# Self attention on one core: the place of the second piece of scores, of the exps, and the engine that copies first

## The chip, the cores and the metric

The kernel runs on one core of a Trainium2 chip. A core has engines that each work through a queue of their own, in order: TensorE (PE; its weight loads are listed as PEld) multiplies matrices, VectorE (DVE) and ScalarE (ACT) work on elements and can read the accumulation memory PSUM, GpSimd (POOL) works on elements in SBUF, and SyncE (SP) issues transfers. They wait for each other by semaphores only. The metric is the device time of one execution in microseconds (us), as a median over runs.

## The reference

An encoder of one layer over a short context (2 x 77 tokens), and a decoder of one layer over 2 x 2048 tokens: causal self attention, cross attention to the encoder's output, and a feed-forward part, each behind a layer norm and with a residual. All in fp32, width 512, 16 heads of 32. The change touches the decoder's self attention alone:

```python
yn = _ln(y, dec_n1_s, dec_n1_b)
y = y + _mha(yn, yn, ..., sb)          # self attention
...
# in _mha, with q, k, v of shape (2, 16, 2048, 32):
scores = jnp.einsum('bhqd,bhkd->bhqk', q, k) / jnp.sqrt(hd)
scores = scores + bias[None]           # relative bias, -inf above the diagonal
attn = jax.nn.softmax(scores, axis=-1)
out = jnp.einsum('bhqk,bhkd->bhqd', attn, v)
```

## The kernel before

The order of all work is written out by hand; no scheduler moves anything. Self attention is cut into 128 units (b, m, g, t): batch b (2), block m of 512 queries (4), group g of four heads (4), and tile t of 128 queries (4). A unit with index i = 4m + t attends to i + 1 tiles of 128 keys, its size: 1 to 4 in block m = 0, 5 to 8 in m = 1, 9 to 12 in m = 2, 13 to 16 in m = 3. The keys of a unit come in pieces of up to four tiles (`pieces`, L304); a size of 13 is cut 4, 4, 3, 2. Work goes through a stream of pieces, two pieces of one unit at a time (a pair).

For each pair, the loop at L1262 does this:

- It makes sure that the unit's scores and exps are issued (L1265 to L1268).
- `turn` (L397): PE transposes the probabilities of the pair, four 128 x 128 tiles into one PSUM bank (L411), and the bank is copied to SBUF as `pts`, by ACT (L417) or DVE (L415). In blocks m > 0 a bank holds one tile of keys for the four heads, so a full pair fills eight banks. The first half of the banks is copied by ACT, the second by DVE (L414). An exp of a later unit is issued behind the fourth bank (L418), and one more at the end (L420).
- If the pair ends its unit, `slot(n + 1)` runs the jobs of that place: a projection of q, k or v, or an output projection (L206, L217, L230, L242: eight matmul instructions each), the division by the softmax sums, and pieces of norm, encoder or cross attention. Their tables are fixed before (L896 to L928).
- One piece of scores is issued if it may be (L1280): its unit is at most two ahead, and writes over the probabilities of a unit whose tiles have been turned that far (`may_score`, L1244).
- One or two exps (L1282).
- `values` (L422): PE multiplies the turned tiles with v into bank 7 (L428).
- Further pieces of scores, as far as they may go, if the pair had two pieces or the block is m = 0 (L1285).

`scores` (L344) takes four banks, one a head; PE fills them with matmuls on 32 rows each (L361), and DVE empties them: without bias for far keys (L370), with the bias and mask for the last two tiles (L377), each with a running maximum, and when the last piece is done the negated maximum (L384). In blocks m > 0 the four exps of the unit (L387, ACT) are then put on a list, `late_exps`, from which `exps(k)` takes the oldest.

All banks but the one of `values` come from one rotation of seven (`bank`, L170): a stretch that asks for a bank gets the one that was asked for seven requests before, and waits until that has been emptied. A bank of transposes is released by its copy, a bank of scores by DVE.

Of the kernel before, what the change touches and what calls it, by code (L numbers as in the profile page):

```python
# [54 lines left out]
def tile_encoder_decoder(ctx: ExitStack, tc: tile.TileContext, ins, out):  # L55
# [93 lines left out]
    with (  # L149
# [20 lines left out]
        def bank():  # L170

            i = count["bank"] % count["banks"]
            count["bank"] += 1
            return psum[:, i, :]

        def in_turn(what, tile):
            i = count[what] % tile.shape[1]
            count[what] += 1
            return tile[:, i, :]
# [138 lines left out]
        units = [(b, m, g, t) for b in range(B) for m in range(NMB) for g in range(NC) for t in range(TB)]  # L318
# [20 lines left out]
        def exps(k):  # L339

            for _ in range(min(k, len(late_exps))):
                late_exps.pop(0)[1]()
# [54 lines left out]
        def turn(pieces):  # L397

            first = units[pieces[0][0]][1] == 0
            loads = []  # L400
            for n, k0, kn in pieces:
                ks = range(k0, k0 + kn)
                if first:
                    loads += [[(n, k, r) for k in ks] for r in range(HC)]
                else:
                    loads += [[(n, k, r) for r in range(HC)] for k in ks]
            for o, load in enumerate(loads):
                pt = bank()
                pts = in_turn("pts", pts_all).rearrange("p (x q) -> p x q", q=P)
                for x, (n, k, r) in enumerate(load):  # L410
                    nc.tensor.transpose(pt[:, ts(x, P)], state[n]["p"][r][:, ts(k, P)], ident)  # L411
                    got[n, k, r] = pts[:, x, :]
                w = len(load) * P
                if o % 2 if first else o >= (len(loads) + 1) // 2:  # L414
                    nc.vector.tensor_copy(pts[:, : len(load), :], pt[:, :w])  # L415
                else:
                    nc.scalar.copy(pts[:, : len(load), :], pt[:, :w])  # L417
                if o == min(3, len(loads) - 1):  # L418
                    exps(1)
            exps(1)  # L420

        def values(n, k0, kn):  # L422
            b, m, g, t = units[n]
            i = m * TB + t
            for k in range(k0, k0 + kn):
                ot = psum[:, 7, :].rearrange("p (t q) -> p t q", q=P)
                for r in range(HC):
                    nc.tensor.matmul(  # L428
                        ot[rows4(r), t, :], vv[:, k, ts(g * HC + r, HD)], got.pop((n, k, r)),
                        start=(k == 0), stop=(k == i),  # L430
                    )
                if t == TB - 1 and k == i:
                    o = ots[b, m, g] = in_turn("oT", oT_all)
                    (nc.vector.tensor_copy if m else nc.scalar.copy)(o, psum[:, 7, :])
# [461 lines left out]
        for x, (b, m) in enumerate(blocks):  # L896
            u = x * NU
            first = m == 0
# [77 lines left out]
        def slot(n):  # L976
            for f in light[n]:
                f()
            for _, run, _ in jobs[n]:
                load_next()  # L980
                run(loaded[ran[0]])
                ran[0] += 1
            if n == 5:
                load_next()
# [35 lines left out]
        def w_1_load(i):  # L1020

            nc.sync.dma_start(w_1[:, :, ts(i, D)], wchunk("dec_ff1_wT", i * D))
# [221 lines left out]
        def may_score():  # L1244

            if at[0] == len(stream):
                return False
            n, k0, kn = stream[at[0]]
            same = n >= 2 and units[n][:2] == units[n - 2][:2]
            return n < 2 or turned_to[n - 2] >= (min(k0 + kn, size[n - 2]) if same else size[n - 2])  # L1250

        def score_next():
            n, k0, kn = stream[at[0]]
            scores(n, k0, kn)
            scored_to[n] = k0 + kn
            at[0] += 1
# [5 lines left out]
        while i < len(stream):  # L1262
            n = stream[i][0]
            pair = [p for p in stream[i : i + 2] if p[0] == n]
            while scored_to.get(n) != size[n]:  # L1265
                score_next()
            while any(u == n for u, _ in late_exps):
                exps(1)  # L1268
            ends = pair[-1][1] + pair[-1][2] == size[n]
            if ends:  # L1270
                for f in ahead[n + 1]:
                    f()
            turn(pair)
            if n == end - 2:
                for _, k0, _ in pair:
                    w_1_load(k0 // 4)
            turned_to[n] = pair[-1][1] + pair[-1][2]
            if ends and n + 1 < end:
                slot(n + 1)
            if may_score():  # L1280
                score_next()
            exps(2 if units[n][1] == 1 else 1)  # L1282
            for p in pair:
                values(*p)
            while may_score() and (len(pair) > 1 or units[n][1] == 0):  # L1285
                score_next()
            i += len(pair)

        xt_ring += [sb.tile([P, D], F32, name="xt", tag="xt", bufs=2) for _ in range(2)]
# [71 lines left out]
```

## Time and profile before

| what | value |
|---|---|
| time, median of 3 runs | 2931.29 us (2929.42 to 2933.62) |
| profiled execution | 2935.85 us, of which its span is 2934.1 us |
| mean granted TensorE clock in it | 0.991 |
| PE busy | 2868.7 us (98%) |
| DVE busy | 2205.3 us (75%) |
| ACT busy | 1219.5 us (42%) |
| block m = 1, b = 1 (1058 to 1253 us) | PE 192.08, DVE 161.35, ACT 106.23 of 195 us |
| block m = 2, b = 1 (1253 to 1486 us) | PE 231.48, DVE 196.74, ACT 134.87 of 233 us |
| block m = 3, b = 1, without its end (1486 to 1720 us) | PE 231.22, DVE 199.88, ACT 142.73 of 234 us |
| behind self attention (1800 to 2934 us) | PE 1108.90, DVE 768.68, ACT 253.51 of 1134 us |

The span is cut by the blocks of self attention, which fill about the first 1780 us; the encoder and the first cross attention are spread between them. Busy time of PE is generous: matmuls overlap and their ends are modelled, so a PE that stands still for half a microsecond between two matmuls may be shown as busy. What PE lost is read from the distances between the starts of its rows in the timeline, and who ended a wait from the bracket at a row's end.

### The profile page before, as it was taken

Reading aid. Unit: us, or ns where it says so; the run is one execution under the profiler, and the core shown is the slowest. Engines: PE = TensorE matmul, PEld = TensorE weight load, DVE = VectorE, ACT = ScalarE, POOL = GpSimd, SP = SyncE. Lnnn points to the kernel's source line nnn. Section 1 sums busy time; section 2 is a strip of 40 time slices with the busy share of each in tenths; the row PEclk is TensorE's granted clock in tenths of the full one; section 3 lists DMA queues with packets and bytes.
Section 4 is the critical chain, followed back from the end, with each engine's and each line's share of the span. In section 5 each row is a group of like instructions: output and inputs, shape, how many; then the busy total and the mean of one; then the engine's idle time right before and its main releaser. Section 6 shows DMA issues by size and latency. Waiting matters only on the chain.

```text
span 2934.1 us, 60690 instructions
## 1 busy us (share of the span) xinstructions
PE 2868.7 (98%) x24440; PEld 2012.8 (69%) x24440; DVE 2205.3 (75%) x6171; ACT 1219.5 (42%) x2211; POOL 736.9 (25%) x601
## 2 busy tenths in 40 slices
PE   8899999999999999999999999999999899999999
PEld 5457666666666556666666667777777777777788
DVE  4767688878987788888888895767676767676765
ACT  3344456546665445565556672313131313131311
POOL 0100000000000101000000004555555464646465
PEclk9899999999999999999999999999999999999999
DMA  6413301201112502211101115000001000000000
GB/s 174 99 54 112 100 16 56 63 16 44 34 41 64 135 19 76 70 30 56 48 16 37 41 46 191 1 29 1 29 1 38 10 29 1 29 1 29 1 15 15
DMA packets 117644, 137.10 MB, mean 47 GB/s; under 512 B 18241, under 2 KB 73073, under 8 KB 117235
## 3 DMA queue, kind: packets, MB, share of 16 engines
q1 hardware_dynamic: 117362, 133.22, 15.7%
q8 instruction: 192, 3.15, 0.4%
q14 instruction: 90, 0.73, 0.1%
HBM read 111.33 MB, written 21.86 MB: 45 GB/s over the span
## 4 chain that ended last, share of the span: by engine, by line
PE 80%; DVE 13%; issue 2%; POOL 2%; ACT 2%; DMA 1%; SPq 0%; POOLq 0%; DVEq 0%; ACTq 0%
PE psum L1165 13%; PE psum L411 12%; PE psum L361 10%; PE psum L1134 8%; PE psum L428 7%; DVE pp L370 5%; PE psum L230 4%; PE psum L814 4%; PE psum L754 4%; PE psum L206 4%; PE psum L242 4%; PE psum L217 3%; DVE pp L377 3%; PE psum L794 2%; PE psum L805 1%
## 5 line engine op out<-in xcount | busy, mean ns | idle before, releaser
L387 ACT ACTIVATE pp<-pp,nm 128x128 f32<-128x128 f32 (+15 forms) x512 | 614.1, 1209 | 195.1 <-DVE nm L384 192.3
L370 DVE TENSOR_SCALAR_CACHE_REDUCE pp<-psum 128x512 f32<-128x512 f32 (+3 forms) x1024 | 558.0, 589 | 53.3 <-PE psum L361 51.5
L411 PE MATMUL psum<-ident,pp 128*128 128x128 f32 x4352 | 549.0, 279 | 18.0 <-DVE mx L377 11.8
L411 PEld LDWEIGHTS psum<-ident,pp 128*128 128x128 f32 x4352 | 474.5, 142 | 132.4 <-DVE pp L370 57.1
L417 ACT COPY pts<-psum 128x512 f32<-128x512 f32 (+3 forms) x592 | 298.7, 577 | 510.5 <-PE psum L411 401.3
L1117 POOL TENSOR_TENSOR vv<-pp 128x512 f32<-128x512 f32 x320 | 414.5, 1311 | 145.3 <-PE psum L1134 125.7
L361 PE MATMUL psum<-kT,q 32*128 32x512 f32 (+3 forms) x2560 | 353.5, 579 | 8.7 <-DVE mx L377 3.9
L415 DVE COPY pts<-psum 128x512 f32<-128x512 f32 (+2 forms) x544 | 329.9, 660 | 42.5 <-PE psum L411 40.8
L428 PEld LDWEIGHTS psum<-pts,vv 128*32 128x32 f32 x8704 | 226.2, 110 | 123.9 <-issue 116.9
L428 PE MATMUL psum<-pts,vv 128*32 128x128 f32 x8704 | 278.9, 276 | 0.0
L276 POOL TENSOR_TENSOR rstd<-rstd,mhalf 128x1 f32<-128x1 f32 x32 | 18.2, 570 | 919.9 <-DVE rstd L275 854.7
L1154 ACT ACTIVATE kT<-kT,vecs 128x256 f32<-128x256 f32 x256 | 115.2, 499 | 300.8 <-DVE kT L1151 300.8
L377 DVE CUSTOM_DVE_ANT_0 pp<-psum,bias 128x256 f32<-128x256 f32 (+1 forms) x512 | 209.6, 409 | 24.5 <-PE psum L361 16.6
L1151 DVE TENSOR_TENSOR kT<-kT,psum 128x512 f32<-128x512 f32 x256 | 166.4, 680 | 80.9 <-PE psum L1134 80.5
L361 PEld LDWEIGHTS psum<-kT,q 32*128 32x128 f32 x2560 | 119.6, 184 | 153.0 <-issue 99.3
L1165 PE MATMUL psum<-vv 128*128 128x256 f32 x768 | 176.9, 381 | 0.0
L1134 PE MATMUL psum<-oT,vv 128*128 128x256 f32 x736 | 166.5, 380 | 0.0
L1165 PEld LDWEIGHTS psum<-vv 128*128 128x128 f32 x768 | 143.1, 190 | 26.8 <-issue 9.5
L1134 PEld LDWEIGHTS psum<-oT,vv 128*128 128x128 f32 x736 | 138.8, 190 | 24.4 <-issue 6.2
L1117 DVE TENSOR_TENSOR vv<-kT 128x512 f32<-128x512 f32 x160 | 140.0, 892 | 10.8 <-PE psum L1165 9.8
L257 POOL TENSOR_TENSOR xr<-xr,row_dec_sa_out_b 128x512 f32<-128x512 f32 x30 | 38.1, 1274 | 375.1 <-DVE pts L415 244.3
L206 PE MATMUL psum<-nT,wqk 128*128 128x512 f32 x256 | 119.1, 609 | 0.0
(178 smaller groups left out, 3920.0 us busy)
## 6 DMA issues: line engine op xcount, KB each, us to landing
wqk<-in_dec_sa_in_wT_dram SPq DMA_DIRECT2D x64, 256.0 KB, 3.8
bias<-tz SPq DMA_DIRECT2D x128, 128.0 KB, 3.5
wbig<-in_dec_sa_in_wT_dram SPq DMA_DIRECT2D x8, 1024.0 KB, 7.3
vv<-in_enc_ff_wT_dram SPq DMA_DIRECT2D x8, 1024.0 KB, 5.4
wbig<-in_dec_sa_out_wT_dram SPq DMA_DIRECT2D x8, 1024.0 KB, 7.5
vv<-y SPq DMA_DIRECT2D x32, 256.0 KB, 3.5
out_dram<-vv SPq DMA_DIRECT2D x32, 256.0 KB, 2.0
xt<-in_x_dram SPq DMA_DIRECT2D x30, 256.0 KB, 3.9
```

What stands on the lines that cost most here:

```text
L206: nc.tensor.matmul(mm, w[:, c, :], nTs[b, m][:, c, :], start=(c == 0), stop=(c == NC - 1))
L361: nc.tensor.matmul(banks[r][:, : kn * P], q[rows4(r), ts(t, P)], kT[rows4(r), g, k0 * P : (k0 + kn) * P], start=True, stop=True,)
L370: nc.vector.tensor_scalar(p[:, k0 * P : (k0 + far) * P], s[:, : far * P], 1.0, None, ALU.mult, ALU.max, accum_out=st["mx"][:, r, c : c + 1],)
L377: nc.vector.tensor_tensor_reduce(p[:, (i + 1) * P - w : (i + 1) * P], s[:, far * P : kn * P], biases[b, m, g][:, r, 2 * P - w :], 1.0, LOW ...
L387: nc.scalar.activation(p, p, AF.Exp, bias=nm, accum_out=to)
L411: nc.tensor.transpose(pt[:, ts(x, P)], state[n]["p"][r][:, ts(k, P)], ident)
L415: nc.vector.tensor_copy(pts[:, : len(load), :], pt[:, :w])
L417: nc.scalar.copy(pts[:, : len(load), :], pt[:, :w])
L428: nc.tensor.matmul(ot[rows4(r), t, :], vv[:, k, ts(g * HC + r, HD)], got.pop((n, k, r)), start=(k == 0), stop=(k == i),)
L1117: engine.tensor_tensor(dst, quarter(*parts[0], n), quarter(*parts[2], n), SIGN[parts[1]])
L1134: nc.tensor.matmul(mm[:, ts(f, TOK)], a[:, c, ts(f, P)], b[:, c, :], start=(c == 0), stop=(c == 1))
L1165: nc.tensor.matmul(mm[:, t, :], lhs[:, c, ts(t, P)], rhs[:, c, :], start=(n == 0 and c == 0), stop=(n == 3 and c == 1),)
```

## The change

Two places are edited. In `turn`, for blocks m > 0, DVE copies the first half of the banks (rounded down) and ACT the rest, where ACT had the first half (rounded up) and DVE the rest; the number of copies of each engine stays. The exp that stood behind the fourth bank is left for block m = 0 only, so for m > 0 one exp instead of two is issued in `turn`, behind all copies. In the loop, the further pieces of scores come ahead of `values`, directly behind the first piece and its exps, and one exp is issued behind them.

```diff
@@ turn
                 w = len(load) * P
-                if o % 2 if first else o >= (len(loads) + 1) // 2:
+                if o % 2 if first else o < len(loads) // 2:
                     nc.vector.tensor_copy(pts[:, : len(load), :], pt[:, :w])
                 else:
                     nc.scalar.copy(pts[:, : len(load), :], pt[:, :w])
-                if o == min(3, len(loads) - 1):
+                if first and o == len(loads) - 1:
                     exps(1)
             exps(1)
@@ the loop over the stream
             if may_score():
                 score_next()
             exps(2 if units[n][1] == 1 else 1)
+            while may_score() and (len(pair) > 1 or units[n][1] == 0):
+                score_next()
+            exps(1)
             for p in pair:
                 values(*p)
-            while may_score() and (len(pair) > 1 or units[n][1] == 0):
-                score_next()
             i += len(pair)
```

## The prediction

> **What bounds the kernel now.** I read the page's busy times and chain first, then the busy time of each block, then one repeating stretch of block m = 3 row by row on PE, DVE and ACT. The page:
>
> ```profile
> PE 2868.7 (98%) x24440; PEld 2012.8 (69%) x24440; DVE 2205.3 (75%) x6171; ACT 1219.5 (42%) x2211; POOL 736.9 (25%) x601
> PE 80%; DVE 13%; issue 2%; POOL 2%; ACT 2%; DMA 1%; SPq 0%; POOLq 0%; DVEq 0%; ACTq 0%
> 1486.00:1720.00 234.00, 231.22 (x2722) 156.58 (x2715) 199.88 (x644) 142.73 (x199) 5.10 (x4) 0.99 0.12 37
> ```
>
> PE is the bound on average, but the chain goes over to DVE for 13%, and in block m = 3 (third line: length, then PE, PEld, DVE, ACT, POOL busy) DVE is busy for 85%. Such a DVE is not idle at every moment at which PE needs it. The repeating stretch, from the first score piece of one unit's second pair to the next such piece (start, length, line, count), PE:
>
> ```profile
> 1600.15 1.14 PE L361 MATMUL psum<-kT,q 32*128 32x512 f32 x8
> 1601.22 1.30 PE L428 MATMUL psum<-pts,vv 128*32 128x128 f32 x40
> 1602.45 0.93 PE L361 MATMUL psum<-kT,q 32*128 32x384 f32 x8
> 1603.31 4.47 PE L411 MATMUL psum<-ident,pp 128*128 128x128 f32 x32
> 1607.71 1.14 PE L361 MATMUL psum<-kT,q 32*128 32x512 f32 x8
> 1608.78 1.95 PE L428 MATMUL psum<-pts,vv 128*32 128x128 f32 x64
> 1610.66 1.14 PE L361 MATMUL psum<-kT,q 32*128 32x512 f32 x8
> 1611.73 2.84 PE L411 MATMUL psum<-ident,pp 128*128 128x128 f32 x24
> 1614.41 3.70 PE L217 MATMUL psum<-nT,wqk 128*128 128x512 f32 x8
> 1618.04 0.71 PE L361 MATMUL psum<-kT,q 32*128 32x512 f32 x4
> ```
>
> and DVE and ACT in the same stretch:
>
> ```profile
> 1601.31 0.69 DVE L370 TENSOR_SCALAR_CACHE_REDUCE pp<-psum 128x512 f32<-128x512 f32 x1 [0.30 <-PE psum L361]
> ...
> 1606.66 0.16 DVE L384 TENSOR_REDUCE nm<-mx 128x1 f32<-128x5 f32 x1
> 1606.74 2.48 DVE L415 COPY pts<-psum 128x512 f32<-128x512 f32 x4
> 1609.14 0.68 DVE L370 TENSOR_SCALAR_CACHE_REDUCE pp<-psum 128x512 f32<-128x512 f32 x1
> ...
> 1611.82 0.69 DVE L370 TENSOR_SCALAR_CACHE_REDUCE pp<-psum 128x512 f32<-128x512 f32 x1 [0.16 <-PE psum L361]
> ```
>
> ```profile
> 1604.00 2.05 ACT L417 COPY pts<-psum 128x512 f32<-128x512 f32 x4 [6.08 <-PE psum L411]
> 1605.91 1.93 ACT L387 ACTIVATE pp<-pp,nm 128x1920 f32<-128x1920 f32 x1
> ```
>
> The reader is to see that DVE runs without a gap from 1601.31 to 1611.58: eight evictions of scores, four copies, the next evictions. PE loses only 0.76 us here (transposes 4.40 from start to start, 3.64 where nothing waits, as at 1567.71): it always has something that needs no DVE. It is ACT's early copies that free banks 0 to 3 of the transposes, and `values` that fills PE while DVE empties the first piece.
>
> **The change, part by part.** *Fewer score stretches.* A piece of four key tiles takes 1.07 from start to start, one of three 0.86: 0.215 a tile and 0.21 a stretch beside. In the built order the stretches of L361 fall from 299 to 185, so at most 114 x 0.21 = 24 us are saved, where PE doesn't wait otherwise. A rule of the Trainium skill bears on this (TensorEngine Tiling (Array Packing), Key Properties): a change of tiling mode drains TensorE; by it alone the change would give 2931 - 24 = 2907. The same page (PSUM Bottleneck) warns that tiling speeds TensorE up but not the emptying of PSUM, for which both ScalarE and VectorE should be used; the rows here, 1.07 us to fill four banks and 2.45 us for DVE to empty them, agree with that one, and it speaks against two pieces in a row.
>
> *Copies and order in the first pair of a unit in m = 3.* On the clock of the rows above. With the second piece directly behind the first, `values` starts at 1600.15 + 0.86 + 0.65 + 0.21 = 1601.87, the transposes 0.21 earlier, at 1603.10. DVE's evictions keep their times and end at 1606.74. The seventh bank of transposes waits for the last of them, as before; the eighth takes the bank of the first one, now copied by DVE at 1606.74 + 0.60 (four copies fill 2.40), plus 0.07 to resume: transposes end at 1607.41 + 0.45 = 1607.86 (before 1607.71). The next score piece takes the banks of transposes 2 to 5. Three of these are now DVE's: free at 1607.94, 1608.54 and 1609.14, where ACT freed them by 1606. There is no projection in this place to cover it. Its third head starts at 1609.21. DVE evicts the first head when it is ready, 1.16 after its start (1600.15 to 1601.31), so from 1609.17, and frees it at 1609.78. The second piece's fourth head needs just that bank: 1609.85 + 0.86 + 0.21 = 1610.92. Only then `values` starts (before 1608.78); with 1.88 the transposes of the next pair start at 1612.80 instead of 1611.73: **1.07 us lost**. Queued behind the waiting scores on PE are `values`, the transposes and the projection; ACT waits for these transposes, DVE for the projection, where it has slack. Bounds: if the copies freed banks without delay, 1607.86 + 1.93 + 1.88 = 1611.67, 0.06 gained; if the two pieces don't overlap at all, 1609.21 + 1.07 + 1.07 + 1.88 = 1613.23, 1.5 lost. I take 1.07, since the rows show heads overlapping. The other three tiles t, with last pieces of 0.88 or 0.53 a head, give 1.0, 0.7 and 1.0 by the same steps; mean 0.95. Three groups a block are in this steady state: 2 x 12 x 0.95 = **+23**.
>
> *Block m = 2.* Here a first pair is often followed by two more pieces:
>
> ```profile
> 1405.19 0.93 PE L361 MATMUL psum<-kT,q 32*128 32x384 f32 x8
> 1406.05 1.96 PE L428 MATMUL psum<-pts,vv 128*32 128x128 f32 x64
> 1407.93 3.29 PE L361 MATMUL psum<-kT,q 32*128 32x512 f32 x16
> 1411.15 1.09 PE L411 MATMUL psum<-ident,pp 128*128 128x128 f32 x8
> ```
>
> The 3.22 of the third row is 1.29 over 2 x 0.86 + 0.21: DVE-bound already. Three pieces in a row need twelve banks of seven. DVE, continuous from its copies, evicts the first piece from about 1406.1 to 1409.1 and the first head of the second by 1409.7; the third piece's fourth head takes that bank, ends at 1409.7 + 0.07 + 0.86 + 0.21 = 1410.8, `values` 1412.7 and not 1411.15: 1.5 lost, four times a batch. The unit of size 11, behind an eviction of 4 x 0.88, loses 1.0 (three times), that of size 12, behind 4 x 0.53, gains its 0.2. At the borders of the block the runs of three lose 3.2 in all, the run of five ahead of m = 3 gains 1.1, since `values` then covers the last evictions. A batch: 6.0 + 3.0 - 0.6 + 2.1 = 10.5; both **+21**. Bounds: nothing lost beyond the runs of three (+6 a batch) and 1.5 in every unit (16 a batch).
>
> *Block m = 1* has a projection between its transposes and its scores, which hides the copies; without it the 0.95 of m = 3 would hold. The transposes' waits there (0.64 and 0.85 of sizes 6 and 7) are for DVE's evictions, which keep their times: they stay, or pass to the projection's bank. I take 0.25 gained a group, 2 in all. Where the projection is a k that ACT evicts, three exps instead of two follow it; 3 x 1.02 + 0.69 + 0.3 is 0.6 more than the 3.4 us until the next transposes, in three units a batch: 4 lost. **+2** (bounds -8 and +8).
>
> *Exps* are ACT instructions alone, two each; no DMA moves, and SP's and POOL's queues keep their order. In m = 2 and 3 three exps stay in each first pair and the fourth in the next; ACT is busy 61% and the last ends before the next unit's transposes. Only at the end, without scores or projections, the exp behind the copies is late: **+1.5**. The copy of `oT` (L434, 0.6) falls behind the second piece's evictions; that is in the size-16 figure.
>
> **Sum**: 23 + 21 + 2 + 1.5 = 47.5. The profiled execution, 2935.85 with 1.75 around its span, would be 2983.3. It lies 4.6 above the median, so I predict 2978.7, rounded 2978.
>
> **Rivals.** *DVE keeps up* (faster): if scores behind each other start DVE early enough that it is idle when the transposes begin, the 24 us come in, and with them the waits of transposes: 1.69 in each of six groups of m = 3 and 1.49 in each of eight of m = 1, 22 us: 2931 - 46 = 2885. For it: PEld's waits for DVE at L411 sum to 94 us. Against it: DVE has no gap in the stretch shown, and starting a piece earlier ends nothing earlier. It decides from the point where DVE is done about 2 us ahead of the transposes. *About even*: the heads overlap more than I think, the m = 3 loss falls to its lower bound and the saved stretches pay for m = 2: 2931 - 1 + 12 - 8 = 2934. *ACT becomes late*: next transposes wait for an exp behind the copies, about 1 us in each of 32 units of m = 1: 2963; against it ACT's 54% there. *Heavier*: upper bounds throughout, 36 + 32 + 8 + 2: 3009. That the change doesn't do what it says is excluded by the built order.
>
> **Numbers.** Forecast 0.71; DVE keeps up 0.08; about even 0.06 (a third of it each way); ACT late 0.06; heavier 0.09. The forecast's own range is 2950 to 3000, half to one and a half of the price; with the even and the heavy case's nearer halves 2943 to 3005. A change of under 0.2%, 6 us, can't be told from none here. Faster 0.08 + 0.02, within 0.02, slower the rest, 0.88.
>
> **What would show it.** In the after trace, PE's score stretches of m = 3's first pairs should be 2.5 to 3.1 long instead of 1.93, with DVE pts L415 as what ended their waits (3.3 us in all now, over 15 then); first transposes should start 0.2 earlier and end about where they did; ACT's copies lie in the second half of a turn. Blocks m = 2 and 3 should each be some 10 to 15 us longer, m = 1 within 4, the part behind self attention unchanged. It is wrong if DVE shows gaps ahead of its first copies, if the waits come from ACT, or if m = 3 is no longer than before.

## The result, and the profile after

The changed kernel takes 3034.76 us (median of 4 runs, 3029.29 to 3036.24) against 2932.41 us of the kernel before in the same comparison: ratio 1.0343, 95% interval 1.033 to 1.0356, some 102 us slower. Its profiled execution took 3036.24 us (span 3034.5), 100.4 more than the one of before.

The page of the changed kernel: busy times, then two of the costliest groups (busy and mean ns of one, then the idle time of the engine ahead of them and what ended most of it). Set apart is the line of L361 from the page of the kernel before:

```profile
PE 2967.9 (98%) x24440; PEld 2102.0 (69%) x24440; DVE 2205.1 (73%) x6171; ACT 1229.2 (41%) x2211; POOL 737.5 (24%) x601
...
L387 ACT ACTIVATE pp<-pp,nm 128x128 f32<-128x128 f32 (+15 forms) x512 | 613.9, 1205 | 572.2 <-DVE nm L384 563.6
...
L361 PE MATMUL psum<-kT,q 32*128 32x512 f32 (+3 forms) x2560 | 449.7, 571 | 12.6 <-DVE pp L370 4.7
```

```profile
L361 PE MATMUL psum<-kT,q 32*128 32x512 f32 (+3 forms) x2560 | 353.5, 579 | 8.7 <-DVE mx L377 3.9
```

The instructions are the same in number, and VectorE's and ScalarE's busy time has hardly moved. PE is "busy" for 99 us more, and 96 of these stand in one group: the score matmuls at L361, 353.5 us before and 449.7 now, for the same 2560. They wait, and a wait between pipelined matmuls is largely shown as busy. ScalarE's exps now sit idle for 572 us until VectorE has the maxima (195 before), since all scores come earlier relative to the exps that use them. That idle time costs nothing.

The waits of PE's weight loads say for whom (us in total, times, longest), in the changed kernel and then in the one before:

```profile
PEld psum L361 <- DVE pp L370: 64.8, 126, 0.8
PEld psum L361 <- DVE pts L415: 26.7, 104, 0.3
...
PEld psum L411 <- DVE mx L377: 12.7, 41, 2.2
```

```profile
PEld psum L411 <- DVE pp L370: 57.1, 88, 1.5
...
PEld psum L361 <- DVE pp L370: 14.0, 39, 0.8
```

Before, scores waited 14.0 us for DVE's evictions at L370 and 3.3 for its copies at L415, while the transposes waited 57.1 us for L370 and 36.5 for L377; now they wait 4.3 and 12.7. The waits have moved from the transposes to the scores, and have grown on the way.

PE in block m = 3, the unit whose stretch stands in the prediction (start, length, line, count):

```profile
1684.87 2.82 PE L361 MATMUL psum<-kT,q 32*128 32x512 f32 x16
1687.62 1.30 PE L428 MATMUL psum<-pts,vv 128*32 128x128 f32 x40
1688.85 4.00 PE L411 MATMUL psum<-ident,pp 128*128 128x128 f32 x32
1692.80 3.18 PE L361 MATMUL psum<-kT,q 32*128 32x512 f32 x16
1695.91 1.95 PE L428 MATMUL psum<-pts,vv 128*32 128x128 f32 x64
1697.79 2.84 PE L411 MATMUL psum<-ident,pp 128*128 128x128 f32 x24
1700.47 3.60 PE L217 MATMUL psum<-nT,wqk 128*128 128x512 f32 x8
1704.00 3.03 PE L361 MATMUL psum<-kT,q 32*128 32x512 f32 x16
```

From the first row to the last it is 19.13 us, where it was 17.89. Both score stretches are too long. The one at 1692.80, behind transposes, is the first pair that the prediction worked out. The one at 1684.87 lies behind a projection, where the banks of the last transposes had been free for 3 us or more: four tiles and three should take 0.86 + 0.65 + 0.21 = 1.72 from start to start, and take 2.75. What holds it is seen best where the trace splits the stretch, here at the start of m = 2, PE and then DVE:

```profile
1277.44 1.61 PE L361 MATMUL psum<-kT,q 32*128 32x512 f32 x14
1279.35 0.69 PE L361 MATMUL psum<-kT,q 32*128 32x256 f32 x2 [0.30 <-DVE pp L370]
1279.97 1.95 PE L428 MATMUL psum<-pts,vv 128*32 128x128 f32 x64
```

```profile
1278.60 0.69 DVE L370 TENSOR_SCALAR_CACHE_REDUCE pp<-psum 128x512 f32<-128x512 f32 x1 [0.30 <-PE psum L361]
1279.21 0.69 DVE L370 TENSOR_SCALAR_CACHE_REDUCE pp<-psum 128x512 f32<-128x512 f32 x1
```

Fourteen matmuls are seven heads. The eighth head needs an eighth bank of a rotation of seven: the one that the first head took, which VectorE starts to empty 1.16 us after the stretch began and frees 0.61 later. The eighth head starts at 1279.35, and `values` at 1279.97 instead of 1278.94 (0.86 + 0.43 + 0.21 behind the start): 1.03 late, although the row's bracket shows 0.30. All 95 stretches of two pieces in blocks m = 1 to 3 are longer than 0.215 a tile and 0.21 a stretch by 0.90 to 1.19 us, whatever lies ahead of them.

By block, from the stretch with a block's first scores to the next block's: m = 1 is 9.3 and 10.8 us longer (b = 0 and 1), m = 2 18.9 and 18.6, m = 3 19.4 and 20.7, together 97.7 of the 100.4. What follows self attention is about 3 longer.

### The profile page after: what moved, and what is told of

It is laid out like the page before. It is cut to its first block, busy times and chain, and to the rows that moved or that the text cites. A ratio compares the mean times of both kernels' runs of the same rounds, so it can differ in the third digit from the quotient of the medians.

```text
span 3034.5 us, 60596 instructions
## 1 busy us (share of the span) xinstructions
PE 2967.9 (98%) x24440; PEld 2102.0 (69%) x24440; DVE 2205.1 (73%) x6171; ACT 1229.2 (41%) x2211; POOL 737.5 (24%) x601
## 3 DMA queue, kind: packets, MB, share of 16 engines
q8 instruction: 192, 3.15, 0.4%
## 4 chain that ended last, share of the span: by engine, by line
PE 82%; DVE 12%; issue 2%; POOL 2%; DMA 1%; ACT 1%; SPq 0%; POOLq 0%; DVEq 0%; ACTq 0%
PE psum L1165 13%; PE psum L411 12%; PE psum L361 12%; PE psum L1134 8%; PE psum L428 7%; DVE pp L370 4%; PE psum L230 4%; PE psum L814 4%; PE psum L754 4%; PE psum L206 4%; PE psum L242 4%; PE psum L217 3%; DVE pp L377 2%; PE psum L794 2%; DVE pts L415 1%
## 5 line engine op out<-in xcount | busy, mean ns | idle before, releaser
L370 DVE TENSOR_SCALAR_CACHE_REDUCE pp<-psum 128x512 f32<-128x512 f32 (+3 forms) x1024 | 555.4, 590 | 78.7 <-PE psum L361 75.2
L411 PE MATMUL psum<-ident,pp 128*128 128x128 f32 x4352 | 530.1, 277 | 7.5 <-DVE mx L377 2.9
L361 PE MATMUL psum<-kT,q 32*128 32x512 f32 (+3 forms) x2560 | 449.7, 571 | 12.6 <-DVE pp L370 4.7
L361 PEld LDWEIGHTS psum<-kT,q 32*128 32x128 f32 x2560 | 201.5, 185 | 238.2 <-issue 95.5
L415 DVE COPY pts<-psum 128x512 f32<-128x512 f32 (+2 forms) x544 | 329.4, 659 | 30.3 <-PE psum L411 28.6
L428 PEld LDWEIGHTS psum<-pts,vv 128*32 128x32 f32 x8704 | 232.8, 112 | 116.3 <-issue 104.3
L428 PE MATMUL psum<-pts,vv 128*32 128x128 f32 x8704 | 289.6, 281 | 1.6 <-ACT pts L417 0.7
L377 DVE CUSTOM_DVE_ANT_0 pp<-psum,bias 128x256 f32<-128x256 f32 (+1 forms) x512 | 209.6, 409 | 22.5 <-PE psum L361 15.1
```

The source lines that it names most:

```text
L361: nc.tensor.matmul(banks[r][:, : kn * P], q[rows4(r), ts(t, P)], kT[rows4(r), g, k0 * P : (k0 + kn) * P], start=True, stop=True,)
L370: nc.vector.tensor_scalar(p[:, k0 * P : (k0 + far) * P], s[:, : far * P], 1.0, None, ALU.mult, ALU.max, accum_out=st["mx"][:, r, c : c + 1],)
L377: nc.vector.tensor_tensor_reduce(p[:, (i + 1) * P - w : (i + 1) * P], s[:, far * P : kn * P], biases[b, m, g][:, r, 2 * P - w :], 1.0, LOW ...
L428: nc.tensor.matmul(ot[rows4(r), t, :], vv[:, k, ts(g * HC + r, HD)], got.pop((n, k, r)), start=(k == 0), stop=(k == i),)
```

## The experiments

Three theories were on record. A: a stretch of two pieces asks for eight banks where seven rotate. B: the prediction's, VectorE's late copies hold the banks of the next scores. C: ScalarE is late. The first three kernels make one part of the change each. In kernels with an added line ahead of `scores`, L361 is shown as L362 and so on.

**The order alone.**

```diff
             exps(2 if units[n][1] == 1 else 1)
+            while may_score() and (len(pair) > 1 or units[n][1] == 0):
+                score_next()
             for p in pair:
                 values(*p)
-            while may_score() and (len(pair) > 1 or units[n][1] == 0):
-                score_next()
```

> Only the order of the pieces is changed; copies and exps stay as before. Theory A (too few banks): a stretch of two pieces asks for eight banks where seven rotate, so the second piece's fourth head must wait until VectorE has emptied the first piece's first head, 1.16 + 0.61 + 0.07 us after the stretch began; every two-piece stretch lasts 2.96 us instead of 1.93, and nearly the whole loss is here: 3015 to 3035 us, score stretches of 2.96 also in block m = 1 and behind projections. Theory B (the prediction's): the scores wait for transposed banks that VectorE copies late; with ScalarE's early copies back the loss is gone: 2915 to 2945 us.

Measured: 3027.47 us (3024.78 to 3033.01), ratio 1.032 (1.0304 to 1.0335), 93 slower. A stretch behind a projection in m = 3, with ScalarE still copying first:

```profile
1700.84 3.03 PE L361 MATMUL psum<-kT,q 32*128 32x512 f32 x16
1703.80 1.52 PE L428 MATMUL psum<-pts,vv 128*32 128x128 f32 x48
```

2.96 instead of 1.93, the same as in the changed kernel, without any late copy. Theory A's interval was met. The order alone costs nearly as much as the whole change.

**The copies alone.**

```diff
-                if o % 2 if first else o >= (len(loads) + 1) // 2:
+                if o % 2 if first else o < len(loads) // 2:
```

> Only the halves of the copies are exchanged: VectorE the first, ScalarE the rest; scores and exps stay in their old places. Theory A: the banks of scores don't change, what is lost is only the late release of the first transposed banks in first pairs of blocks m = 2 and 3, up to 1 us in a unit where VectorE is behind: 2940 to 2970 us. Theory B: most of the 102 us: 2985 to 3030 us. Either way block m = 1 should keep its length within 3 us.

Measured: 3031.28 us (3029.77 to 3032.57), ratio 1.0328 (1.0311 to 1.0346), 97 slower. In m = 3, a first pair:

```profile
1604.13 2.32 PE L361 MATMUL psum<-kT,q 32*128 32x512 f32 x8
1606.38 1.95 PE L428 MATMUL psum<-pts,vv 128*32 128x128 f32 x64
1608.27 1.14 PE L361 MATMUL psum<-kT,q 32*128 32x512 f32 x8
```

The first piece takes 2.25 from start to start where it took 1.07: it finds the banks of the early transposes still to be copied. The second piece, behind `values`, has its 1.07. For VectorE's copies at L415 scores now wait 43.1 us (3.3 before). Theory A is missed by far, and theory B's upper end by 1 us; block m = 1, which was to keep its length within 3 us, is 7.6 and 8.2 longer. So the copies are dear by themselves too, in another place: with the exps below, the parts sum to 93 + 97 + 15 = 205 us, and all three at once cost 102. Order and copies seem to make PE wait for one and the same chain of VectorE work, and the wait is paid once; the kernel without fourth heads below bears this out.

**The exps alone.**

```diff
-                if o == min(3, len(loads) - 1):
+                if first and o == len(loads) - 1:
                     exps(1)
@@
             exps(2 if units[n][1] == 1 else 1)
+            exps(1)
```

> Only the exps move: none behind the fourth copy in blocks m > 0, one more behind the first piece of scores. Theories A and B: no more than 5 us from before, 2928 to 2938 us. Theory C (ScalarE becomes late): transposes of the next unit wait for exps, 2950 us or more, with ACT pp L387 as what ends waits at L411.

Measured: 2949.86 us (2948.16 to 2951.27), ratio 1.0052 (1.0037 to 1.0067), 15 slower, nearly all in m = 2. PE and then ACT there:

```profile
449.05 3.75 PE L411 MATMUL psum<-ident,pp 128*128 128x128 f32 x32
452.73 2.00 PE L361 MATMUL psum<-kT,q 32*128 32x512 f32 x8
454.66 1.61 PE L428 MATMUL psum<-pts,vv 128*32 128x128 f32 x50
```

```profile
449.03 1.26 ACT L387 ACTIVATE pp<-pp,nm 128x1152 f32<-128x1152 f32 x1 [4.50 <-DVE nm L384]
...
450.29 1.24 ACT L387 ACTIVATE pp<-pp,nm 128x1152 f32<-128x1152 f32 x1
...
451.53 2.02 ACT L417 COPY pts<-psum 128x512 f32<-128x512 f32 x4
```

Two exps, issued behind the first piece, wait for a maximum that VectorE makes only at 449.03, and ScalarE's copies of the next turn stand behind both: they start 2.48 us after the transposes, where before one exp stood ahead of them and they started 1.24 after. The next scores take 1.93 instead of 1.07. ScalarE is late here, as theory C had it, but not by the sign that it named: transposes wait 3.1 us for exps (5.0 before), and scores 9.4 us for ScalarE's copies (4.1 before). My step that put the exps at nothing is wrong for them alone.

**The eighth bank taken away.** In the order-only kernel, the pieces that come behind a first piece leave out their fourth head: no matmuls and no bank, while VectorE empties the third head's bank a second time, so that its work stays. The control is the kernel before with the same heads left out.

```diff
-            banks = [bank() for _ in range(HC)]
-            for r in range(HC):
+            banks = [bank() for _ in range(heads)]
+            banks += banks[-1:] * (HC - heads)
+            for r in range(heads):
@@
             while may_score() and (len(pair) > 1 or units[n][1] == 0):
-                score_next()
+                score_next(HC - 1)
```

> The order alone, as in e1, but the pieces that follow directly leave out the scores of their fourth head: no matmul and no bank for it, and VectorE empties the third head's bank once more in its place, so VectorE's work is the same and a two-piece stretch asks for seven banks. Theory A (the eighth bank): two-piece stretches fall from 2.96 to about 1.93, block m = 1 loses nothing any more; only the runs of three pieces in m = 2 still wait; 2930 to 2960 us. Theory D (the order costs because values no longer stands between score pieces and VectorE has to follow at once): 3010 us or more, as in e1.

> The kernel before with the same scores left out in the same pieces (fourth head of each piece behind values; VectorE empties the third head's bank once more): the control of e4. Heads of a piece run side by side, so nothing should be saved: 2915 to 2935 us under every theory.

Measured: 2951.39 us with the order changed (ratio 1.0059, 1.0039 to 1.0079) and 2925.76 for the control (0.9972, 0.9961 to 0.9982). The order's price falls from 93 to 25.6: some 67 us hang on the eighth bank. The control is itself 9 us faster than the kernel before: there too runs of two pieces behind `values` ask for eight banks, and what L361 takes over its unhindered length in m = 2 falls from 8.8 to 1.4 us a batch. With the order changed, the stretch that took 2.96:

```profile
1629.45 2.04 PE L362 MATMUL psum<-kT,q 32*128 32x512 f32 x14
1631.42 1.52 PE L429 MATMUL psum<-pts,vv 128*32 128x128 f32 x48
```

1.97, where two pieces of four tiles without a wait take 1.93. What stays is 12 us a batch over the control in m = 2 and m = 3 together, most of it in m = 2 and at the border between them, where runs of three pieces ask for ten banks of seven even so. Block m = 1, which was to lose nothing, is 0.6 shorter and 3.9 longer.

**The same with the whole change.** The heads are left out as above.

> The changed kernel, all three parts, with the fourth head of the pieces that come behind a first piece left out (no matmuls, no bank; VectorE empties the third head's bank once more), so that a stretch of two asks for seven banks and not eight. Its control is the kernel before with the same heads left out (2925.76). Theory A (the eighth bank is most of the price): two four-tile pieces in a row fall from 2.96 us to about 1.7, and what stays is the runs of three in m = 2 (25.6 in the order-only pair) and the first pairs in m = 3 that wait for VectorE's late copies (at most 24 groups x 1.5 = 36): 2950 to 2985. Theory B (the late copies hold the banks in all stretches, the eighth bank is only where it shows): 3000 to 3030, and first pairs in m = 3 stay at 2.5 to 3.1 us.

Measured: 3000.07 us (2999.12 and 3001.01), ratio 1.0231 (1.021 to 1.0251); 74 over the control. Theory A missed its interval, and B's lower end was hit. With the late copies in place the eighth bank is worth only 102 - 74 = 28 us. This is the unit that begins at 1704.00 in the changed kernel's rows:

```profile
1670.96 2.03 PE L362 MATMUL psum<-kT,q 32*128 32x512 f32 x14
1672.92 1.52 PE L429 MATMUL psum<-pts,vv 128*32 128x128 f32 x48
1674.37 2.84 PE L412 MATMUL psum<-ident,pp 128*128 128x128 f32 x24
1678.03 1.46 PE L412 MATMUL psum<-ident,pp 128*128 128x128 f32 x8 [0.81 <-DVE mx L378]
1679.42 3.17 PE L362 MATMUL psum<-kT,q 32*128 32x512 f32 x14
1682.53 1.95 PE L429 MATMUL psum<-pts,vv 128*32 128x128 f32 x64
...
1691.06 1.60 PE L362 MATMUL psum<-kT,q 32*128 32x384 f32 x14
```

The stretch behind the projection takes 1.96 where it took 2.96. But VectorE begins the copies 7.12 us behind the start of that stretch in both kernels, and the transposes, which wait for its evictions ahead of them, now take 5.05 instead of 4.05. The first pair takes 3.11 for seven heads as it took 3.12 for eight, and the unit 20.10 in both. What the eighth bank no longer costs here, the transposes lose. In m = 3 of b = 0 this holds, nearly, for three of a group's four units; the fourth loses 0.4 us instead of 1.5. Either cause alone suffices for most of the loss; neither may be called "the" share of it.

**VectorE first in the ending pairs only**, which mostly have a projection behind their transposes, with the order as before.

```diff
+                ends = pieces[-1][1] + pieces[-1][2] == units[n][1] * TB + units[n][3] + 1
-                if o % 2 if first else o >= (len(loads) + 1) // 2:
+                if o % 2 if first else o < len(loads) // 2 if ends else o >= (len(loads) + 1) // 2:
```

> The copies alone, as in e2, but VectorE copies first only in pairs that end their unit, which a projection follows; first pairs of blocks m = 2 and 3 keep ScalarE first. If the price of e2 is the late release of transposed banks to the scores that follow at once, it stays in the first pairs and goes: 2935 to 2960 us, block m = 1 as in e2 (about 8 us a batch, from transposes and projections that wait for the first copies). If VectorE's first copies cost wherever they are: 2980 us or more.

Measured: 2966.05 us (2963.48 to 2967.31), ratio 1.0108 (1.0093 to 1.0123), 31.5 slower, a little over what was expected. First pairs, without cover, make up 97 - 31.5 = 65 us of the copies' price. The rest is partly in m = 1, 8 to 9 us a batch (here and below a block is measured from its first `values` to the next block's): no score waits there, but the transposes lose 3 us a batch more, and where the jobs begin with transposes of cross attention (L794) and no projection, these ask for a bank at once. The changed kernel shows it too:

```profile
1190.56 1.86 PE L794 MATMUL psum<-ident,pp 128*77 128x128 f32 x12 [1.06 <-DVE pts L415]
```

**Jobs between the two pieces.** The order alone, but in m = 1 and 3 the unit's jobs stand between its first and its second piece of scores.

```diff
-            if ends and n + 1 < end:
+            between = units[n][1] in (1, 3)
+            if ends and n + 1 < end and not between:
                 slot(n + 1)
@@
             exps(2 if units[n][1] == 1 else 1)
+            if ends and n + 1 < end and between:
+                slot(n + 1)
```

> The order of the change alone, but with the unit's jobs (a projection in most units) moved in m = 1 and 3 from ahead of the first piece to between the first piece and the second, so that VectorE has 3.5 us for the first piece's four evictions before the second piece asks for its eighth bank. Base: the order alone, 3027.47, of which the runs with three heads put 67 us on the eighth bank, over m = 1, 2 and 3. Theory A (the second piece waits for the first one's eviction because nothing lies between them): the two-piece stretches behind projections fall back to 1.07 and 1.07 in m = 1 and 3; first pairs and m = 2 keep theirs: 2975 to 3000. Rival: the first piece, now directly behind the transposes, waits for their copies, and what the second gains the first loses: 3015 to 3035.

Measured: 2992.53 us (2989.49 to 2998.58), ratio 1.0208 (1.0191 to 1.0225), 35 less than the order alone, with the same banks and the same VectorE work:

```profile
1659.34 1.14 PE L361 MATMUL psum<-kT,q 32*128 32x512 f32 x8
1660.41 3.70 PE L217 MATMUL psum<-nT,wqk 128*128 128x512 f32 x8
1664.04 1.14 PE L361 MATMUL psum<-kT,q 32*128 32x512 f32 x8
1665.11 1.52 PE L428 MATMUL psum<-pts,vv 128*32 128x128 f32 x48
```

Both pieces take 1.07. Against the order alone, m = 1 gains 10.8 and 12.5 us, and the rest lies in m = 3 and at the borders of m = 2, which keeps its price; this is theory A for the order alone, shown without leaving anything out. What fills PE between two pieces is what counts there.

**The kernel before, with the jobs last**: in m = 1 and 3 they come behind the last scores instead of ahead of the first.

```diff
+        LATE = (1, 3)
@@
+            late = units[n][1] in LATE
-            if ends and n + 1 < end:
+            if ends and n + 1 < end and not late:
                 slot(n + 1)
@@ behind the further pieces of scores
+            if ends and n + 1 < end and late:
+                slot(n + 1)
```

> The kernel before, with the jobs of a unit's end (projection, division, norm pieces) put behind the last scores instead of ahead of the first, in blocks m = 1 and 3. If transposes wait only because VectorE is still emptying the last piece (0.6 to 0.9 us in half of the units), 3.5 us of projection between the two hide that: 5 to 20 us faster than before, 2912 to 2927 us. If the projection is needed where it is, to cover the copies ahead of the first piece, the scores wait instead: 2930 to 2950 us.

Measured: 2914.49 us (2913.6 to 2915.02), ratio 0.9932 (0.9917 to 0.9947): 20 us faster than the kernel before, and the fastest kernel of this study.

```profile
1579.75 0.93 PE L361 MATMUL psum<-kT,q 32*128 32x384 f32 x8
...
1581.10 3.60 PE L206 MATMUL psum<-nT,wqk 128*128 128x512 f32 x8
1584.54 3.66 PE L411 MATMUL psum<-ident,pp 128*128 128x128 f32 x32
1588.12 1.14 PE L361 MATMUL psum<-kT,q 32*128 32x512 f32 x8
```

The 32 transposes take 3.58 where the same place took 4.40 before: the projection now covers VectorE's last evictions, for which transposes waited. Three ways to go further failed. With at most one further piece of scores in all blocks m > 0:

> l1, and behind values at most one further piece of scores in blocks m > 0, so that no run of two or four pieces is left. If runs wait for banks that VectorE empties (1.29 us in four runs of two a batch, 5.3 us in the run of four), m = 2 gets 5 us shorter a batch and the border to m = 3 about 5: 2895 to 2908 us. If VectorE's work is the bound there whatever the order: within 4 us of l1's 2914.

Measured: 3138.74 us (ratio 1.07, 1.0682 to 1.0718), far outside both intervals. The runs of two in m = 2 lose their waits, but in m = 3 scores fall a piece behind and exps come right ahead of the transposes that need them:

```profile
PEld psum L411 <- ACT pp L387: 210.9, 143, 4.1
```

With that limit in m = 2 alone:

> The kernel before with late jobs in m = 1 and 3 and, in m = 2 alone, at most one further piece behind values. Theory A (too few banks): the runs of two behind values, 1.29 us each, some four to seven a batch, are gone: 2900 to 2912. Rival: scores then fall behind, exps come right ahead of their transposes as they did in m = 3 when the cap was put on all blocks, and m = 2 gains nothing: 2914 to 2930.

Measured: 2920.12 us (ratio 0.9959, 0.9944 to 0.9974), some 6 over the late jobs alone, as the rival had it: m = 2 is 1 us a batch shorter, and transposes wait 20.4 us for VectorE's negated maxima (L384) and 15.5 for exps instead. With the jobs last in m = 2 as well:

> The kernel before with the unit's jobs behind its last scores in m = 2 as well as in m = 1 and 3. In m = 2 the transposes lose 3.5 us a batch to waits and a run of two four-tile or three-tile pieces behind values 1.29 us each; jobs behind the last scores can hide the first, not the second. Theory A: 4 to 7 us below the late jobs in m = 1 and 3 alone (2914.5), 2907 to 2911. Rival: the jobs covered the first score piece's wait for copies in m = 2, which now shows: 2915 to 2930.

Measured: 2933.03 us (ratio 1.0003, 0.9993 to 1.0012), outside both intervals. In m = 2 the jobs had covered the copies of a unit's short last turn, and now nothing does:

```profile
517.85 1.48 PE L361 MATMUL psum<-kT,q 32*128 32x256 f32 x8
519.26 0.64 PE L428 MATMUL psum<-pts,vv 128*32 128x128 f32 x16
520.26 0.42 PE L428 MATMUL psum<-pts,vv 128*32 128x128 f32 x8 [0.35 <-DVE pts L415]
```

Scores of two tiles take 1.41 instead of 0.64, and `values` waits for its turned tiles.

## Why the prediction was right in direction and wrong in size

*What bounds the kernel.* Right: the price is PE standing for VectorE, with both engines' work unchanged.

*The steps that failed.* There are two. The first is the one that read "`values` starts at 1600.15 + 0.86 + 0.65 + 0.21 = 1601.87": a stretch of two behind a projection was added up without a wait. On the changed kernel's clock that unit starts at 1684.87, and `values` at 1687.62 and not at 1686.59. The rule needed was in my own text, "the second piece's fourth head needs just that bank", and I applied it only where the copies were late. It holds wherever two pieces follow each other: 1.16 until VectorE begins, 0.61 for the first eviction, against 1.07 for PE to fill four banks. For the order alone, the experiments with three heads (67 of 93 us) and with the jobs between the pieces (35 us) show it. In the whole change it can account for at most 28 us of the 55 that the prediction lacks, since 74 of the 102 stay without the fourth heads.

The second is "a projection between its transposes and its scores, which hides the copies", which put block m = 1 at +2. The scores indeed wait for nothing there with the copies alone, but the block is 7.6 and 8.2 us longer all the same: its transposes take 3.1 and 3.4 us more, and its jobs 4.4 and 5.1. Over the whole run the jobs' matmuls at L294 and L695, which no projection covers, now wait 6.9 us for VectorE's copies at L415, and did not before.

*The terms of the sum.* Per block, both batches, predicted and measured: m = 1 +2 and 20.1; m = 2 +21 and 37.5; m = 3 +23 and 40.1. Beside the 47.5 that I summed stand 100.4. Without the second pieces' fourth heads, and against the control, they are 16.5, 24.5 and 35.2, and 73.3 in all: m = 2 is then near what I had, m = 1 and m = 3 are not.

- In m = 1 nearly every unit has its stretch of two behind a projection or other jobs, which are no answer to the eighth bank: in b = 0, L361 is over its unhindered length (0.215 a tile and 0.21 a stretch) by 16.0 us in 16 stretches, where it was by 0.1. The block's 9.3 us there can be followed: 15.9 more at L361, less 4.9 of waits at the transposes, less 16 x 0.21 = 3.4 for the stretches saved, plus 1.6 in the cross attention's own rows, whose transposes have no projection ahead of them. With the eighth bank out of the way the loss doesn't go, it moves: L361 is then 2.3 us below the control, the transposes 3.5 and the jobs 5.1 above it, and the block 6.3 longer. Either cause makes m = 1 longer by itself.
- In m = 3 the length of the first pair was right: 3.06 worked out (1607.86 to 1610.92), 3.11 measured. That it came from "the second piece's fourth head" was not: without that head first pairs still take 3.1 (in one unit of four 2.58), so the late copies suffice for it. The wait behind the projection is largely won back in the same unit, since the transposes that follow take 3.95 from start to start and not the 4.76 I had. That unit loses 1.24 where I had 1.07. The mean of 0.95 was too small: in the first three groups of b = 0 each unit behind the block's first loses 1.15 to 1.64.
- In m = 2 the runs of three are too long, as I had it: the four of b = 0 take 5.72 us each, 3.15 over the unhindered length, where the runs of two of before were 1.29 over. Without the fourth heads the block loses 11.3 and 13.2 us, where I had 10.5; with them, 18.9 and 18.6.

*Exps at nothing.* Wrong alone (15 us), because ScalarE's queue is in order and a waiting exp holds its copies. In the changed kernel, exps are not what transposes wait for: 0.9 us in all, 5.0 before.

*The saved stretches.* They did come in, as the sum for m = 1 shows, and so did most of the transposes' waits for evictions (57.1 + 36.5 us before, 4.3 + 12.7 now), on which the rival "DVE keeps up" counted. Both were paid for several times over at L361: that rival saw the waits rightly, but its condition, a VectorE that is done early, was not met. "ACT late" is excluded as the main cause; "heavier", at 3009, took all my upper bounds and was still too low: m = 1 at +8 had neither an eighth bank nor the copies' price, and m = 2 and m = 3 are over their upper bounds of 32 and 36 too. By the drain rule of the Trainium skill (TensorEngine Tiling (Array Packing), Key Properties) the change should have gained; the same page's PSUM Bottleneck section pointed the right way, and this case's rows agree with it: 1.07 us for PE to fill four banks, about 2.45 for VectorE to empty them.

*The signs.* Scores wait for L415 as I had it, 26.7 us where I wanted over 15. Blocks m = 2 and m = 3 were to be 10 to 15 us longer and m = 1 within 4, and all three are over that. I had not looked for the 64.8 us at L370.

*Additivity.* I summed the parts as if each had its own wait. The one-part kernels show 93, 97 and 15 for a whole of 102.

## What to carry to other kernels

Before two bursts that fill accumulation banks are put next to each other, count the banks they ask for against the rotation; if there is one more than rotates, the second burst runs at the pace of the engine that empties the first one, however free the banks were ahead of it. What to put between two bursts is work that needs no bank of the rotation, or few of them: the same order with a projection between the pieces got 35 us back, and jobs moved behind the last scores in the kernel before gained 20. Where an engine that empties banks is behind in other work too, as with the late copies here, a wait taken from one place comes back at the next: 28 us were left of the eighth bank's 67. Parts of one edit that wait for the same chain don't add up, so test each alone before believing a sum.

## What the runs showed of the hardware that was not expected

In one kernel the granted clock fell where PE kept pausing. In the kernel with at most one further piece, these are 20 us windows of b = 0 around the border from m = 2 to m = 3 (length, then PE, PEld, DVE, ACT and POOL busy; granted clock; DMA share and GB/s), and two rows of transposes from PE's timeline in the first and the second of them:

```profile
600.00:620.00 20.00, 19.21 (x255) 12.82 (x253) 16.50 (x51) 10.01 (x16) 0.00 (x0) 1.00 0.16 41
620.00:640.00 20.00, 14.61 (x109) 10.25 (x112) 9.52 (x33) 10.19 (x14) 0.00 (x0) 0.83 0.05 14
```

```profile
613.67 3.38 PE L411 MATMUL psum<-ident,pp 128*128 128x128 f32 x29 [0.79 <-ACT pp L387]
...
634.37 5.20 PE L411 MATMUL psum<-ident,pp 128*128 128x128 f32 x29 [1.19 <-ACT pp L387]
```

With PE busy for 96% the clock is 1.00 and 29 transposes take 3.38 us; behind four pauses of 1.2 to 1.5 us it is 0.83 and they take 5.20. Over that whole run the mean is 0.958, against 0.991 of the kernel before. The Trainium skill has such a case (TensorE: Matmul & The Clock Gate, A second HAM failure mode: psum-queue depth-cycling): short pauses between groups of matmuls let the clock swing. These rows agree with it in kind. But the clock doesn't follow a window's busy share alone: from 640 to 660 us PE is busy for 82% at a clock of 0.97, and from 680 to 700 for 93% at 0.85. And no run here shows how much of that kernel's 204 us is clock and how much is waiting. The changed kernel's mean clock is 0.987, 0.4% below that of before, so at most some 12 of its 102 us can lie there.

The second point is how little of a stall a trace admits to: the 1.03 us that a stretch of two loses is shown as a pause of 0.30 where the trace splits the stretch, and as nothing where it doesn't. Only the distance from start to start tells it.
